# Where VectorE makes the split weights of the next chunk in a feed-forward network, and GpSimd's tall third parts in two operations

## The chip, the cores and the metric

The kernel runs on one core of one Trainium2 chip. The metric is the device time of one execution of the program in microseconds (us). The profile also gives the span (from the first to the last instruction in the trace), the busy time of each engine, and the clock that TensorE was granted, as a share of full speed.

The engines of the core work side by side, each in the order of its own instructions: TensorE (PE; its weight loads are shown apart as PEld), VectorE (DVE), ScalarE (ACT), GpSimd (POOL) and SyncE (SP), which issues most of the transfers. An instruction that needs another engine's result waits on a semaphore, and everything behind it in its own engine's order waits too.

## The reference, cut to what matters

A graph network on `x` of 1024 x 512 in fp32: a normalized and rectified `x` goes through a graph convolution (16384 edges), four layers of cross attention and a gated feed-forward network, and a second graph convolution, with residual sums. The change lies in the feed-forward network:

```python
N, D, BS, M, DC, H, DH, L, E = (1024, 512, 16, 256, 512, 8, 64, 4, 16384)
...
for i in range(L):
    a = _attn(_ln(h, ln2_w[i], ln2_b[i]), cond, Wq[i], Wk[i], Wv[i], Wo[i])
    h = h + a
    u = _ln(h, ln3_w[i], ln3_b[i]) @ geglu_w[i] + geglu_b[i]
    val, gate = jnp.split(u, 2, axis=-1)
    f = val * jax.nn.gelu(gate, approximate=False)
    h = h + f @ ffo_w[i] + ffo_b[i]
```

`geglu_w[i]` is 512 x 4096, so `val`, `gate` and `f` are 1024 x 2048; `ffo_w[i]` is 2048 x 512.

## The kernel before

**Tiling.** The large products are made by a scheme that needs seven block products where the plain one needs eight, at the price of sums and differences of blocks before and after. The products are numbered 0 to 6. The 2048 columns of `f` are worked off in four blocks r = 0 to 3 of 512 columns. Each block is made in four chunks c = 0 to 3 of 128 columns (the first product, with `geglu_w`), and later multiplied with its 512 rows of `ffo_w` in two output halves s = 0 and 1 (the second product).

**A chunk.** Block r = 0 is made in plain fp32 by another class. Blocks 1 to 3 use `Chunk` (from L1123), in which six of the seven products are made with split operands: each operand is written as a high part plus a low part in a narrower format (fp32r), and the product is the sum of three narrower ones. `split_left` (L1110) makes the three parts of a weight tile: the high part `gha` or `ghb` on ScalarE (L1112), the low part `gla` or `glb` on VectorE (L1113), and the third part, their difference, `gsa` or `gsb` on GpSimd (L1114). Each chunk has two such tiles: the tall one (names in a), 128 x 1024, holds the blocks of products 0, 5, 6 and 4; the low one (names in b), 128 x 512, those of products 1 and 3. `split(n, False)` splits the tall tile of the nth chunk ahead, `split(n, True)` its low tile. A chunk's weights arrive by transfers that SyncE issues when the chunk is made (L1137), and GpSimd builds the sums of its blocks (L1147, `sum_chunk`).

`Chunk.steps` is a generator that issues one chunk in stages. A product's first two parts are multiplied in `begin` (`gr` with `gha`, then `gl` with `gla`), the third part in `end` (`gr` with `gsa`), all by the matmuls at L1163. Between them ScalarE scales the bank in place (`scale`, L1177), or VectorE scales it and adds a term (`scale_onto`, L1181); VectorE adds (L1198), and ScalarE takes the GELU (L1190). The results go to `fT` (L1229, L1232). The fourth stage ends, in the kernel before, with a call of `split_low`, which the loop gives as `split(0, True)`.

**The right blocks.** The operand that all chunks share, the normalized `h`, is split as well. Its low parts `gl` are made by `finish_right` on VectorE (L1107), two operations for each product, during the last stage of r = 0.

**The output halves.** `Gated.sums` (L1302 to L1310) makes the sums and differences of the `fT` blocks for the second product (`fs`). `ffn_out` (L1320) then issues one half of the second product: seven products of eight matmuls each (L1333) into four banks of PSUM, `fa`, `fb`, `fc` and `fd`. VectorE adds them into the layer's sum `hall` (L1339) and into `kept`, a tile for each half that collects the terms common to several blocks (L1343 and L1351; for r = 0, ScalarE copies into it at L1345). The order is:

- TensorE: product 0 into `fa`, 6 into `fc`, 4 into `fd`, 5 into `fb`, 1 into `fa` again (onto what is there, in the same bank), 3 into `fc` and 2 into `fd`.
- VectorE: `kept` += `fa`, `hall` += `fc`, `hall` += `fd`, `kept` += `fb`, then `hall` += `fa`, += `fc`, += `fd`.

The second use of `fa` must wait until the first `kept` add has read it, that of `fc` until the first `hall` add has read that bank.

**The order of the work.** All of this is pinned: each engine works in the order in which the Python program issues its instructions. The loop over r = 1 to 3 and c = 0 to 3 interleaves the last stages of the chunk before with the first of this one. The two output halves of block r - 1 are issued behind the chunks c = 0 and c = 1 of the blocks r = 2 and 3, those of block 0 ahead of the loop, and those of block 3 in a last stage behind it, which the change doesn't touch. `out_weights` (L216 to L219) makes the sums of the `ffo_w` blocks on GpSimd once a block. SBUF slots and PSUM banks come from pools and are reused in order of allocation.

Of the kernel before, what the change touches and what calls it, by code (L numbers as in the profile page):

```python
# [11 lines left out]
F32R = mybir.dt.float32r  # L12
I32 = mybir.dt.int32
AF = mybir.ActivationFunctionType
OP = mybir.AluOpType
# [10 lines left out]
def gnn_kernel(  # L26
# [26 lines left out]
    nc = tc.nc  # L53
# [43 lines left out]
    def t512(name, dtype=F32):  # L97
        return work.tile([P, 512], dtype, tag="t512", name=name)

    def slot(name):  # L100
        return slots.tile([P, 2, 512], F32, tag="slot", name=name)
# [106 lines left out]
    h = [hall[:, nb, :] for nb in range(NB)]  # L208
# [76 lines left out]
    conds, left = {}, None  # L285
# [68 lines left out]
    at = 0  # L354
# [101 lines left out]
    def project_steps(nb, hT, w, name, emit):  # L456

        ph = bank(f"hw_{name}_{nb}")
        c0 = (nb % 4) * P
        for k in range(KC):  # L460
            nc.tensor.matmul(ph, hT[nb // 4][k // 2][:, k % 2, c0:c0 + P],
                             w[k // 2][:, k % 2, :], start=(k == 0), stop=(k == KC - 1),
                             skip_group_check=True)
            yield
        emit(nb, ph)
# [132 lines left out]
    def add_left(left, rows, to, root, name):  # L598

        for d in range(NB):  # L600
            nc.sync.dma_start(left.rearrange("p a b -> p (a b)"), left_dram[d])
            pl = bank(f"left_{name}_{d}")
            for s in range(NB):
# [7 lines left out]
    steps = (step for nb in range(NB)  # L611
             for step in project_steps(nb, h0T, w_in, "in",
                                       lambda nb, ph: nc.scalar.copy(hs_in[nb], ph)))
# [89 lines left out]
    def acc_tile(name):  # L703
        return accs.tile([P, 512], F32, tag="acc", name=name)
# [385 lines left out]
    pin = tc.keep_in_program_order  # L1090
# [19 lines left out]
    def split_left(x, h, l, s):  # L1110

        pin(nc.scalar.mul(h.bitcast(F32R), x, INWARD * TINY))  # L1112
        pin(nc.vector.scalar_tensor_tensor(l.bitcast(F32R), h, -1.0 / TINY, x, OP.mult, OP.add))  # L1113
        pin(nc.gpsimd.tensor_tensor(s.bitcast(F32R), h, l, OP.subtract))  # L1114

    def columns_of(t):
        return t.rearrange("p (b k c) -> p b k c", k=2, c=P)

    def flat(t):
        return t.rearrange("p a b -> p (a b)")  # L1120

    class Chunk:
# [26 lines left out]
        def split(self, low):  # L1149
            if low:  # L1150
                to = [t512(f"g{n}b_{self.n}") for n in "hls"]
            else:
                to = [flat(slot(f"g{n}a_{self.n}")) for n in "hls"]
            split_left(self.x[low], *to)
            self.parts[low] = [columns_of(t.bitcast(F32R)) for t in to]
# [33 lines left out]
            cg = self.cv + DFF // P  # L1189
            pin(nc.scalar.activation(to, of, AF.Gelu, bias=gcols[:, cg:cg + 1]))  # L1190

        def steps(self, sum_next, split_low):


            n, bias = self.n, gcols[:, self.cv:self.cv + 1]

            def add(to, x, y):
                pin(nc.vector.tensor_tensor(to, x, y, OP.add))  # L1198

            self.banks = {}  # L1200
            self.scale(0)
            self.scale(5)
            yield
            s1, u2, u3 = (acc_tile(f"g{x}_{n}") for x in ("s1", "u2", "u3"))
            pin(nc.scalar.copy(s1, self.end(0)))
            self.scale(6)
            yield
            add(u2, self.end(5), s1)
            yield
            sum_next()  # L1210
            self.scale(4)
            add(u3, self.end(6), u2)
            self.scale_onto(1, s1)
            g1 = acc_tile(f"g1_{n}")
            d = self.end(4)
            add(g1, d, u3)
            self.gate(g1, g1)
            self.scale_onto(3, u3)
            split_low()
            yield  # L1220
            a = self.end(1)
            yield
            g0 = acc_tile(f"g0_{n}")
            self.gate(g0, self.end(3))
            for k in range(2):
                pin(nc.tensor.matmul(d, self.last[:, k, :], self.rights[2][:, k, :], start=False,  # L1226
                                     stop=k == 1, skip_group_check=True))
            f0, f1 = self.f.of(self.c)
            pin(nc.vector.scalar_tensor_tensor(f0, a, bias, g0, OP.add, OP.mult))  # L1229
            add(d, d, u2)  # L1230
            yield
            pin(nc.vector.scalar_tensor_tensor(f1, d, bias, g1, OP.add, OP.mult))  # L1232

    class KeyPair(InStep):
# [3 lines left out]
        x = "k"  # L1238
# [78 lines left out]
        f = Gated(l, r)  # L1317
        return f, [Quad(l, r, c, left, right, f) for c in range(KC)]

    def ffn_out(l, r, s, left, right, kept, each=lambda ins: ins):  # L1320

        n = f"{l}_{r}_{s}"
        u = kept[s]
        a, b, c, d = (bank(f"{x}_{n}") for x in ("fa", "fb", "fc", "fd"))
        h11, h12, h21, h22 = (hall[:, 4 * i + 2 * s:4 * i + 2 * s + 2, j * M:(j + 1) * M]
                              for i in range(2) for j in range(2))

        def product(i, to, start):  # L1330
            for q in range(2):
                for k in range(2):
                    each(nc.tensor.matmul(to[:, q * M:(q + 1) * M],  # L1333
                                          left[i][k][:, (2 * s + q) * P:(2 * s + q + 1) * P],
                                          right[i][:, k, :], start=start and q == 0 and k == 0,
                                          stop=q == 1 and k == 1, skip_group_check=True))

        def add(to, of):
            each(nc.vector.tensor_tensor(to, halves_of(of), to, OP.add))  # L1339

        product(0, a, True)
        if r:
            each(nc.vector.tensor_tensor(u, a, u, OP.add))  # L1343
        else:
            nc.scalar.copy(u, a)  # L1345
        product(6, c, True)
        add(h22, c)
        product(4, d, True)
        add(h22, d)
        product(5, b, True)  # L1350
        each(nc.vector.tensor_tensor(u, b, u, OP.add))  # L1351
        if r == R - 1:
            for to in (h22, h21, h12):
                add(to, u)
        product(1, a, False)
        add(h11, a)
        product(3, c, False)
        add(h21, c)
        product(2, d, False)
        add(h12, d)  # L1360
# [43 lines left out]
    class QueryPair(InStep):  # L1404


        x = "q"
# [134 lines left out]
    for l in range(L):  # L1542

        wk, wv, wq, wo, ffb, spare = projections
        if l:
# [13 lines left out]
            kT_1, _ = keys(l, 1, wk)  # L1559
# [28 lines left out]
        ln3T, ln3S, right = [], [], []  # L1588
# [66 lines left out]
        for g in range(NG - 1):  # L1655
# [11 lines left out]
            if turn_two:  # L1667
                t = turn_next(g + 2)
# [19 lines left out]
            elif g:  # L1688
                turned = range(g) if g == NG - 2 else []
                if turned:  # L1690
                    with waiting_for(scores.last, mybir.EngineType.Pool):
                        left = geglu_weights(l, 0, *raw)
# [38 lines left out]
        f, quads = quads_of(l, 0, left, right)  # L1731
# [24 lines left out]
        kept = [t512(f"kept_{l}_{i}") for i in range(2)]  # L1756
# [7 lines left out]
        def finish_rights(*of):  # L1764
            for i in of:
                x, high, mid = begun[i]
                flow = finish_right(f"gl_{l}_{i}", x, high)
                Chunk.rights[i] = high, next(flow), mid
                yield
                for _ in flow:  # L1770
                    yield
# [13 lines left out]
        for c, q in enumerate(quads):  # L1785
            q.rest(fill)
            if c == 0:
                with waiting_for(q.last, mybir.EngineType.Pool):
                    wff = out_weights(nc.gpsimd, l, 0, raw_out)
# [10 lines left out]
        def sum_chunk(n):  # L1800
            if n < len(ready):
                ready[n].sums()
# [4 lines left out]

        load()
        sum_chunk(0)
        for _ in finish_rights(5, 6):  # L1810
            pass
        ffn_out(l, 0, 0, f.left(), wff, kept, pin)
        split(0, False)
        split(0, True)
        load()
        sum_chunk(1)
        for _ in finish_rights(4, 3):
            pass
        ffn_out(l, 0, 1, f.left(), wff, kept, pin)
        split(1, False)  # L1820
        load()
        raw_out = load_out(l, 1)

        def split_next(n):
            split(n, False)
            load()

        before = None
        for r in range(1, R):
            for c in range(KC):  # L1830
                chunk = ready.pop(0)
                flow = chunk.steps(lambda: sum_chunk(1), lambda: split(0, True))
                chunk.f = f if c else Gated(l, r)
                next(flow)
                if c > 2 or r == 1 and c or r > 1 and c == 0:
                    split_next(0)
                for step in range(3):
                    if before:
                        next(before, None)
                        if step == 2 and c == 0:  # L1840
                            f.sums(KC - 1, nc.vector, pin)
                    next(flow)
                if c:
                    f.sums(c - 1, nc.vector, pin)
                before = flow
                if c == 0:
                    kept_f, f = f, chunk.f
                if r > 1 and c < 2:
                    split_next(1)
                    ffn_out(l, r - 1, c, kept_f.left(), wff, kept, pin)  # L1850
                    if c == 1:
                        raw_out = load_out(l, r)
                if c == (KC - 1 if r + 1 < R else KC - 2):
                    wff = out_weights(nc.gpsimd, l, r, raw_out)
# [162 lines left out]
```

## Time and profile before

| | |
|---|---|
| median of three runs | 2477.06 us (2476.02 to 2477.70) |
| the profiled execution | 2477.45 us, its span 2475.6 us |
| mean granted TensorE clock over the span | 0.992 |
| ScalarE, high parts and scaling among it | 837.2 us busy, 34% |
| GpSimd | 1050.7 us busy, 1079 instructions |
| VectorE's `gla` (L1113), 48 in all | 85.6 us busy, 1784 ns each |
| memory traffic | 138.12 MB read, 23.07 MB written, 65 GB/s over the span |

The page of the profile begins with the busy time of each engine and its share of the span; behind the x is the number of instructions. In a view of waits, a row such as `PE fa L1333 <- DVE kept L1343: 37.8, 8, 4.7` says that TensorE's instructions that write `fa` at line 1333 waited for VectorE's `kept` of line 1343, 37.8 us in total, in 8 waits, the longest of them 4.7. In a timeline, a row gives the start, the duration, the engine, the line, the operation, output and inputs, the shape, how many instructions stand in the row (x8), and in brackets how long its engine idled before it and what ended this. Where a row stands for several matmuls its duration runs from the first's start to the last's end. In a view of windows, a row gives for each stretch its length, the busy time of each engine with the number of instructions, the granted clock (PEclk), and the share and rate of the transfers.

### The profile page before, as it was taken

Reading aid. Unit: us, or ns where it says so; the run is one execution under the profiler, and the core shown is the slowest. Engines: PE = TensorE matmul, PEld = TensorE weight load, DVE = VectorE, ACT = ScalarE, POOL = GpSimd, SP = SyncE. Lnnn points to the kernel's source line nnn. Section 1 sums busy time; section 2 is a strip of 40 time slices with the busy share of each in tenths; the row PEclk is TensorE's granted clock in tenths of the full one; section 3 lists DMA queues with packets and bytes.
Section 4 is the critical chain, followed back from the end, with each engine's and each line's share of the span. In section 5 each row is a group of like instructions: output and inputs, shape, how many; then the busy total and the mean of one; then the engine's idle time right before and its main releaser. Section 6 shows DMA issues by size and latency. Waiting matters only on the chain. (4 is left out here: it accounts for less than half of the span.)

```text
span 2475.6 us, 35108 instructions
## 1 busy us (share of the span) xinstructions
PE 2401.2 (97%) x13032; PEld 1883.8 (76%) x13032; DVE 1701.2 (69%) x3252; ACT 837.2 (34%) x1784; POOL 1050.7 (42%) x1079
## 2 busy tenths in 40 slices
PE   8999999999999999999999999999999999999999
PEld 5778886677787887577787888477787888667787
DVE  9665666877676557886686556776785556777764
ACT  7323344333213334343213334432323333433220
POOL 0433444564453222574453224554544322555531
PEclk9999999999999999999999999999999999999999
DMA  5323220111302220021221221011131031011140
GB/s 178 122 68 116 90 95 18 43 43 52 119 31 77 87 74 20 22 64 43 62 96 69 77 72 41 9 60 43 43 132 69 14 124 48 5 52 39 47 145 35
DMA packets 118065, 163.55 MB, mean 66 GB/s; under 512 B 9256, under 2 KB 66928, under 8 KB 117888
## 3 DMA queue, kind: packets, MB, share of 16 engines
q1 hardware_dynamic: 115792, 155.81, 19.1%
q0 software_dynamic: 1376, 4.30, 0.5%
q8 instruction: 107, 1.75, 0.3%
q10 hardware_dynamic: 720, 1.11, 0.1%
q14 instruction: 70, 0.57, 0.1%
HBM read 138.12 MB, written 23.07 MB: 65 GB/s over the span
## 5 line engine op out<-in xcount | busy, mean ns | idle before, releaser
L1177 ACT ACTIVATE g<-g 128x512 f32<-128x512 f32 x192 | 112.1, 584 | 312.6 <-PE g L1163 308.8
L1114 POOL TENSOR_TENSOR gsb<-ghb,glb 128x512 fp32r<-128x512 f32 x48 | 74.2, 1545 | 240.6 <-DVE glb L1113 240.6
L1333 PE MATMUL fa<-wff,fT 128*128 128x256 f32 x512 | 135.2, 410 | 37.8 <-DVE kept L1343 37.8
L1114 POOL TENSOR_TENSOR gsa<-gha,gla 128x1024 fp32r<-128x1024 f32 x48 | 115.0, 2396 | 111.9 <-DVE gla L1113 111.9
L1333 PEld LDWEIGHTS fa<-wff,fT 128*128 128x128 f32 x512 | 105.1, 207 | 61.1 <-DVE kept L1343 41.0
L799 ACT ACTIVATE pr<-sc,nmax 128x256 f32<-128x256 f32 x256 | 118.2, 471 | 83.1 <-DVE nmax L794 82.6
L1163 PE MATMUL g<-gr,gsa 128*128 128x512 f32 x384 | 136.6, 437 | 0.0
L1003 POOL TENSOR_TENSOR kr<-ct,ct 128x256 f32<-128x256 f32 x48 | 36.8, 766 | 211.8 <-DVE pr L804 207.2
L1190 ACT ACTIVATE g<-g,gcols 128x512 f32<-128x512 f32 x96 | 67.4, 703 | 168.8 <-DVE g L1198 165.6
L300 PE MATMUL pa_v<-wv,ct 128*128 128x256 f32 x512 | 124.0, 385 | 0.0
L1163 PE MATMUL g<-gr,gha 128*128 128x512 f32 x384 | 122.7, 401 | 0.0
L300 PE MATMUL pc_v<-wv,ct 128*128 128x256 f32 x512 | 121.0, 379 | 0.0
L300 PE MATMUL pd_v<-wvs,ct 128*128 128x256 f32 x512 | 121.0, 379 | 0.0
L1163 PE MATMUL g<-gl,gla 128*128 128x512 f32 x384 | 118.6, 390 | 0.0
L794 DVE TENSOR_REDUCE nmax<-sc 128x2 f32<-128x512 f32 x128 | 83.7, 679 | 41.2 <-PE sc L787 41.2
L300 PEld LDWEIGHTS pa_v<-wv,ct 128*128 128x128 f32 x512 | 94.9, 190 | 22.5 <-issue 9.2
L300 PEld LDWEIGHTS pd_v<-wvs,ct 128*128 128x128 f32 x512 | 97.3, 190 | 13.2
L300 PEld LDWEIGHTS pc_v<-wv,ct 128*128 128x128 f32 x512 | 97.0, 190 | 13.0
L1113 DVE SCALAR_TENSOR_TENSOR gla<-gha,gxa 128x1024 fp32r<-128x1024 f32 x48 | 85.6, 1784 | 18.0 <-ACT gha L1112 18.0
L1163 PEld LDWEIGHTS g<-gr,gsa 128*128 128x128 f32 x384 | 71.9, 188 | 33.5 <-issue 16.3
L1229 DVE SCALAR_TENSOR_TENSOR fT<-g,gcols,g 128x512 f32<-128x512 f32 x48 | 35.9, 749 | 80.1 <-ACT g L1190 79.8
L1226 PE MATMUL g<-ln3T,gy 128*128 128x512 f32 x192 | 90.4, 592 | 0.0
(520 smaller groups left out, 6357.5 us busy)
## 6 DMA issues: line engine op xcount, KB each, us to landing
ct<-cond_dram SPq DMA_DIRECT2D x72, 512.0 KB, 5.6
wff<-in_L_gnn_ffo_w_dram SPq DMA_DIRECT2D x32, 512.0 KB, 3.9
cond_dram<-ct SPq DMA_DIRECT2D x24, 512.0 KB, 3.0
gxb<-in_L_gnn_geglu_w_dram SPq DMA_DIRECT2D x96, 128.0 KB, 2.2
gxa<-in_L_gnn_geglu_w_dram SPq DMA_DIRECT2D x96, 128.0 KB, 2.3
cond<-in_L_gnn_cond_dram SPq DMA_DIRECT2D x32, 256.0 KB, 4.7
ct<-cond_dram SPq DMA_DIRECT2D x24, 256.0 KB, 5.6
wk<-in_L_gnn_Wk_dram SPq DMA_DIRECT2D x8, 512.0 KB, 6.3
```

What stands on the lines that cost most here:

```text
L300: each(nc.tensor.matmul(at, left[:, k, l0:l1], right[:, k, r0:r1], start=start and n == 0 and k == 0, stop=n == len(cols_of) - 1 and k == ...
L794: nc.vector.tensor_reduce(nmax, ps3, AX.X, OP.max, negate=True)
L799: nc.scalar.activation(pr3[:, a, :], ps3[:, a, :], AF.Exp, bias=nmax[:, a:a + 1], accum_out=tot[:, a:a + 1])
L1003: t.tensor_tensor(to, of, less, OP.subtract)
L1113: pin(nc.vector.scalar_tensor_tensor(l.bitcast(F32R), h, -1.0 / TINY, x, OP.mult, OP.add))
L1114: pin(nc.gpsimd.tensor_tensor(s.bitcast(F32R), h, l, OP.subtract))
L1163: pin(nc.tensor.matmul(to, self.part(i, which)[:, k, :], self.rights[i][which].bitcast(F32R)[:, k, :], start=start and k == 0, stop=stop a ...
L1177: pin(nc.scalar.mul(to, to, 1.0 + TINY))
L1190: pin(nc.scalar.activation(to, of, AF.Gelu, bias=gcols[:, cg:cg + 1]))
L1226: pin(nc.tensor.matmul(d, self.last[:, k, :], self.rights[2][:, k, :], start=False, stop=k == 1, skip_group_check=True))
L1229: pin(nc.vector.scalar_tensor_tensor(f0, a, bias, g0, OP.add, OP.mult))
L1333: each(nc.tensor.matmul(to[:, q * M:(q + 1) * M], left[i][k][:, (2 * s + q) * P:(2 * s + q + 1) * P], right[i][:, k, :], start=start and q ...
```

## The change

It has four parts.

1. `split_left`: GpSimd makes the third part in column blocks of 512. For the low tile that is one operation as before; for the tall tile, two of 128 x 512 in place of one of 128 x 1024. That adds 48 instructions on GpSimd. ScalarE's and VectorE's operations on the tall tile stay whole.
2. `ffn_out` takes a sequence `beside` of functions. The first is called after VectorE's second `kept` add (for r = 3 after the adds of `u`, too), ahead of product 1; the others after `hall` += `fa`, ahead of product 3.
3. Block r = 0: the right blocks of product 6 are finished inside the first half instead of ahead of it, those of 3 inside the second half, both with the splits that stood behind these halves; those of product 4 are finished inside the second half instead of ahead of it, and only those of product 5 still come ahead of the first.
4. Blocks r = 2 and 3, chunks c = 0 and 1: `split(0, True)` is no longer called in the fourth stage of the chunk, and `split_next(1)` no longer ahead of `ffn_out`; both go into `ffn_out` as `beside`. In all other chunks `split(0, True)` is called at the same place as before.

The instructions of TensorE, ScalarE and SyncE stand in the same order before and after. On VectorE 17 operations a layer stand elsewhere (11 of L1113 and 6 of L1107); on GpSimd, `gsa` and `gsb` follow them, in two pieces where tall.

```diff
@@ split_left
-        pin(nc.gpsimd.tensor_tensor(s.bitcast(F32R), h, l, OP.subtract))
+        for at in range(0, x.shape[-1], 512):
+            h_at, l_at, s_at = (t[:, at:at + 512] for t in (h, l, s.bitcast(F32R)))
+            pin(nc.gpsimd.tensor_tensor(s_at, h_at, l_at, OP.subtract))
@@ Chunk.steps
-        def steps(self, sum_next, split_low):
+        def steps(self, sum_next):
...
             self.scale_onto(3, u3)
-            split_low()
             yield
@@ ffn_out
-    def ffn_out(l, r, s, left, right, kept, each=lambda ins: ins):
+    def ffn_out(l, r, s, left, right, kept, each=lambda ins: ins, beside=()):
...
         if r == R - 1:
             for to in (h22, h21, h12):
                 add(to, u)
+        for do in beside[:1]:
+            do()
         product(1, a, False)
         add(h11, a)
+        for do in beside[1:]:
+            do()
         product(3, c, False)
@@ ahead of the loop (r = 0)
-        for _ in finish_rights(5, 6):
-            pass
-        ffn_out(l, 0, 0, f.left(), wff, kept, pin)
-        split(0, False)
-        split(0, True)
+        def finish(*of):
+            for _ in finish_rights(*of):
+                pass
+
+        def split_both():
+            split(0, False)
+            split(0, True)
+
+        finish(5)
+        ffn_out(l, 0, 0, f.left(), wff, kept, pin, (lambda: finish(6), split_both))
         load()
         sum_chunk(1)
-        for _ in finish_rights(4, 3):
-            pass
-        ffn_out(l, 0, 1, f.left(), wff, kept, pin)
-        split(1, False)
+        ffn_out(l, 0, 1, f.left(), wff, kept, pin,
+                (lambda: finish(4), lambda: (finish(3), split(1, False))))
@@ the loop over r and c
-                flow = chunk.steps(lambda: sum_chunk(1), lambda: split(0, True))
+                flow = chunk.steps(lambda: sum_chunk(1))
...
+                output = r > 1 and c < 2
+                if not output:
+                    split(0, True)
                 if c:
                     f.sums(c - 1, nc.vector, pin)
...
-                if r > 1 and c < 2:
-                    split_next(1)
-                    ffn_out(l, r - 1, c, kept_f.left(), wff, kept, pin)
+                if output:
+                    ffn_out(l, r - 1, c, kept_f.left(), wff, kept, pin,
+                            (lambda: split(0, True), lambda: split_next(1)))
```

## The prediction

> **What bounds the kernel now.** I read the page's first two parts, then the list of TensorE's own waits, then the timelines around the longest of them. All times are from the one profiled execution, which took 2477.45 us (its span 2475.6, 1.85 around it); the median of the runs is 2477.06, 0.39 less.
>
> ```profile
> span 2475.6 us, 35108 instructions
> PE 2401.2 (97%) x13032; PEld 1883.8 (76%) x13032; DVE 1701.2 (69%) x3252; ACT 837.2 (34%) x1784; POOL 1050.7 (42%) x1079
> ...
> PE fa L1333 <- DVE kept L1343: 37.8, 8, 4.7
> PE fd L1333 <- DVE fs L1309: 8.7, 11, 0.9
> PE fc L1333 <- DVE hall L1339: 4.7, 4, 1.2
> ```
>
> TensorE is busy 97% of the span: only what shortens its idle time, or the stretches in which it runs slowly, can count. Its longest wait by far (total, times, longest) is in the output halves: 37.8 us in 8 waits, before the second product into `fa`, on VectorE's `kept` add. Eight is one in each of r = 2 and 3 in four layers: the half that follows chunk c = 0. The next view is the timeline of TensorE there (start, duration), with the half after c = 1 below it:
>
> ```profile
> 539.32 1.56 PE L1333 MATMUL fd<-wffs,fs 128*128 128x256 f32 x6 [0.94 <-DVE fs L1309]
> 540.72 1.89 PE L1333 MATMUL fb<-wffs,fs 128*128 128x256 f32 x8
> 547.34 3.78 PE L1333 MATMUL fa<-wff,fT 128*128 128x256 f32 x8 [4.72 <-DVE kept L1343]
> 555.10 0.81 PE L1163 MATMUL g<-gr,gha 128*128 128x512 f32 x2
> ...
> 572.17 1.89 PE L1333 MATMUL fa<-wff,fT 128*128 128x256 f32 x8
> 573.90 1.89 PE L1333 MATMUL fc<-wffs,fT 128*128 128x256 f32 x8
> 577.17 0.81 PE L1163 MATMUL g<-gr,gha 128*128 128x512 f32 x2
> ```
>
> The wait costs more than its 4.72 us: the eight matmuls into `fa` behind it take 3.78 instead of 1.89. From `fa` to the next chunk's first matmul it is 7.76 us here and 5.00 after c = 1, where nothing waits. The granted clock (PEclk) tells why:
>
> ```profile
> core 0: us, PE busy (x) PEld busy (x) DVE busy (x) ACT busy (x) POOL busy (x), PEclk, DMA share, GB/s
> 544.60:545.60 1.00, 0.00 (x0) 0.00 (x0) 1.00 (x1) 0.00 (x0) 1.00 (x1) 1.00 0.00 0
> 545.60:546.60 1.00, 0.00 (x0) 0.00 (x0) 1.00 (x1) 0.00 (x0) 0.00 (x0) 0.67 0.00 0
> 546.00:547.34 1.34, 0.00 (x1) 0.01 (x1) 1.34 (x3) 0.00 (x0) 0.52 (x1) 0.50 0.00 0
> ...
> 572.17:577.17 5.00, 5.00 (x26) 4.40 (x24) 2.14 (x4) 0.00 (x0) 2.67 (x4) 1.00 0.38 148
> ```
>
> A mean of 0.67 over 545.60 to 546.60 means half speed from about 545.9 on, some 3.3 us after TensorE ran dry at 542.6. The same stretch, `fa` to next chunk, over all eight halves (first, last, sum; the columns are its ends, its length, TensorE's busy time, PEclk and DMA):
>
> ```profile
> 547.34:555.10 7.76, 7.76 (x25) 0.65 0.00 0
> ...
> 2341.77:2348.32 6.55, 6.55 (x24) 0.77 0.00 0
> sum 54.78, PE 54.78; mean PE 6.85
> ```
>
> **The change, part by part.** It adds no work but 48 instructions on GpSimd (each tall third part becomes two); TensorE, ScalarE and SyncE keep their order, VectorE has 17 operations a layer in other places.
>
> *1. `kept` first, in r = 2 and 3.* What VectorE (and GpSimd) did before the late add:
>
> ```profile
> 541.52 0.68 DVE L1198 TENSOR_TENSOR g<-g,gu 128x512 f32<-128x512 f32 x1
> 542.12 0.68 DVE L1181 SCALAR_TENSOR_TENSOR g<-g,gu 128x512 f32<-128x512 f32 x1
> 543.57 0.69 DVE L1113 SCALAR_TENSOR_TENSOR glb<-ghb,gxb 128x512 fp32r<-128x512 f32 x1 [0.76 <-ACT ghb L1112]
> 544.51 2.17 DVE L1113 SCALAR_TENSOR_TENSOR gla<-gha,gxa 128x1024 fp32r<-128x1024 f32 x1 [0.25 <-ACT gha L1112]
> 546.60 0.68 DVE L1343 TENSOR_TENSOR kept<-fa,kept 128x512 f32<-128x512 f32 x1
> ...
> 544.34 1.26 POOL L1114 TENSOR_TENSOR gsb<-ghb,glb 128x512 fp32r<-128x512 f32 x1 [2.55 <-DVE glb L1113]
> ```
>
> The two splits (`glb`, `gla`) and their waits for ScalarE stand between L1181 and `kept`. Both now come later. Operations of this size follow at 0.60 us (541.52, 542.12), so `kept` starts at 542.12 + 0.60 = 542.72 instead of 546.60: 3.88 us earlier, 8 times, **31.0 us**. What is late next: `kept` ends 0.68 later, TensorE could have started at 542.45 (`fb` begins at 540.72, and groups of eight follow at 1.73: 572.17, 573.90), so about 0.84 of the 4.72 stays.
>
> *2. The slow clock.* A wait of 0.84 us ends 2.4 us before the 3.3 at which the clock fell. The waits of 0.94 (`fd` above) and 1.18 (below) were followed by groups of eight at 1.89 and 1.99 us. I take the slow stretch as gone: 54.78 - 8 x 5.00 = **14.8 us**; the other bound is 0.
>
> *3. r = 0.* In the second half of r = 0 VectorE made `gl` for products 4 and 3 ahead of the half's adds:
>
> ```profile
> 475.30 1.89 PE L1333 MATMUL fc<-wff,fT 128*128 128x256 f32 x8
> 483.55 1.99 PE L1333 MATMUL fc<-wffs,fT 128*128 128x256 f32 x8 [1.18 <-DVE hall L1339]
> ...
> 476.12 6.77 DVE L1107 SCALAR_TENSOR_TENSOR gl<-ln3S,gr 128x512 fp32r<-128x512 f32 x4
> 482.82 0.68 DVE L1339 TENSOR_TENSOR hall<-fc,hall 128x512 f32<-128x512 f32 x1
> ```
>
> With them behind the adds, the add of `fc` can run at 475.30 + 1.89 = 477.2, five us before TensorE wants `fc` back (483.55 - 1.18 = 482.37). The wait goes, in four layers: **4.7 us**. `gl` for product 4 now follows `fb`, which is done at 475.30 + 2 x 1.73 + 1.89 = 480.7; two operations of 0.60, or of 1.7 if hindered as in the row (6.77 / 4), end by 484.1, and the next chunk starts only at 482.37 + 2 x 1.73 = 485.8. The splits of r = 0's first half move ahead of its last two adds; nothing on TensorE waits for these.
>
> *4. Tall third parts in two.* [...]
>
> ```profile
> 535.24 2.35 POOL L1114 TENSOR_TENSOR gsa<-gha,gla 128x1024 fp32r<-128x1024 f32 x1
> 535.32 2.82 DVE L1308 TENSOR_TENSOR fs<-fT,fT 128x512 f32<-128x512 f32 x1
> 538.17 1.10 DVE L1309 TENSOR_TENSOR fs<-fs,fT 128x512 f32<-128x512 f32 x1
> ...
> L1114 POOL TENSOR_TENSOR gsa<-gha,gla x48: 2348/2374/2667, 475.7 to 2363.6; 128x1024 fp32r<-128x1024 f32 x48
> L1114 POOL TENSOR_TENSOR gsb<-ghb,glb x48: 1260/1607/1715, 478.4 to 2382.8; 128x512 fp32r<-128x512 f32 x48
> ```
>
> `gsb` is the nearest row to a half of `gsa`: 1.26 to 1.71 us, so a pair is 2.52 to 3.43 against 2.37 (0.15 to 1.06 more, 48 times, on an engine 42% busy). The first `fs` then waits for the first half only: it ends at 535.24 + 1.26 + 0.60 = 537.1 instead of 538.1; the second `fs` meets the second half (to 537.1 + 1.26 = 538.4) and ends near 539.0 instead of 539.27. I take 0.2 us of this as reaching `kept`, 8 times, **1.6 us**. Bounds: 1.09 each, the full difference of 2.35 and 1.26 (8.7 us), and, if both halves go first, a loss of 2.52 - 2.35 = 0.17 each (1.4 us).
>
> [...]
>
> *What hides the moved work.* The tall part is due late, and the banks as well:
>
> ```profile
> 519.53 2.38 POOL L1114 TENSOR_TENSOR gsa<-gha,gla 128x1024 fp32r<-128x1024 f32 x1 [1.16 <-DVE gla L1113]
> 526.66 0.62 PE L1163 MATMUL g<-gr,gsa 128*128 128x512 f32 x2
> ...
> 560.44 0.75 DVE L1229 SCALAR_TENSOR_TENSOR fT<-g,gcols,g 128x512 f32<-128x512 f32 x1 [4.26 <-ACT g L1190]
> 561.60 0.63 PE L1163 MATMUL g<-gr,gha 128*128 128x512 f32 x2
> 570.16 0.68 DVE L1343 TENSOR_TENSOR kept<-fa,kept 128x512 f32<-128x512 f32 x1
> ```
>
> In an ordinary chunk `gsa` is done 4.75 us before its matmul: a pair costs at most 1.06 of it. In a half after c = 0, VectorE's new order is `kept` (542.72), two adds, the second `kept`, `glb`, an add (five steps of 0.60 to 0.70 from 543.3, so to 546.7), `gla`, two adds. `gla` waits for `gsb`, which can start at 546.0 and takes up to 1.71, and itself takes 1.1 (2.17 less the 1.09 that `gsb` held it above): to 548.8, and the adds to about 550.1. The next chunk starts at 543.46 + 5.00 = 548.46, 1.6 us earlier. VectorE is idle for 4.26 there, and the fourth bank of that chunk (product 4, 561.60 - 555.10 = 6.5 us in) is the first that needs one of them. After c = 1, `kept` ends at 570.84 and TensorE comes for it at 572.17: no wait to gain. SyncE's loads in the moved step keep their place in its queue, and what they fill is first used a chunk later. All this I cost at nothing.
>
> Sum: 31.0 + 14.8 + 4.7 + 1.6 = 52.1; 2477.45 - 52.1 = 2425.35, and 0.39 less for the median: **2425 us**.
>
> **The rivals.** *The clock stays slow.* The halves still hold two short waits (0.94 and 0.84) within four us. If these keep the clock down, part 2 is lost: 2425 + 14.8 = 2440. For it: they come closer together than any waits in the rows above. Against it: each alone left the pace unchanged. [...]
>
> *`kept` doesn't come earlier*, because something else on VectorE holds it (its input `fa` is complete before `fd` resumes at 539.32, so I see nothing). Only part 3 is left: 2477.06 - 4.7 = 2472, which is at the edge of what a measurement tells from no change (0.2%, 5 us).
>
> *Slower: the adds behind `gla` come too late.* The place is the first matmul of product 4 after each of the 16 changed halves of r = 2 and 3. If a backlog keeps the last adds from ending within 6.5 us of the chunk's start, TensorE waits there; a wait like today's costs 4.72 + 14.8 / 8 = 6.6 us with its slow clock. 16 x 6.6 = 105 us: 2425 + 105 = 2530. From 3.3 us a half on it eats the gain. Against it: the backlog I find is 1.6 us.
>
> **How the numbers follow.** Forecast 0.78; clock stays slow 0.11; nothing but part 3, 0.04; slower 0.07. Faster is the first two, 0.89; the same 0.04. The forecast's own range is 2425 - (8.7 - 1.6) = 2418 to 2425 + 1.6 + 1.4 = 2428. For eight in ten the first rival is taken in: 2417 to 2441.
>
> **What would show it.** Right: the wait of `fa` on `kept` falls from 4.7 to about 0.8 each; the stretch `fa` to next chunk is 5.0 in all eight halves, with PEclk 1.00; the wait of `fc` on `hall` is gone; `gsa` x96 at 1.26 to 1.71; the first `fs` ends after some 1.8 instead of 2.82. Wrong: PEclk below 1 in these halves (first rival), a new wait of a `g` product on `hall` or on `gsa` (third), or `kept` still starting 4 us after the last L1181.

## The result, and the profile after

The changed kernel takes 2421.68 us (median; 2421.45 to 2422.37) against 2476.70 us for the kernel before: a ratio of 0.9778, with a 95% interval of 0.9761 to 0.9795. The forecast was 2425, with a range of 2417 to 2441.

The page of the profile after, its first lines:

```profile
span 2419.5 us, 35192 instructions
PE 2385.1 (99%) x13032; PEld 1874.2 (77%) x13032; DVE 1665.3 (69%) x3252; ACT 838.0 (35%) x1784; POOL 1050.1 (43%) x1127
```

The span is 56.1 us shorter. TensorE's idle time went from 74.4 us (2475.6 - 2401.2) to 34.4, its busy time from 2401.2 to 2385.1: 40.0 us of waits and 16.1 us of slow work. The list of TensorE's waits of the kernel after begins with:

```profile
PE fa L1334 <- DVE kept L1344: 6.7, 8, 0.8
PE fd L1334 <- DVE fs L1310: 4.4, 11, 0.4
```

`fa` on `kept` fell from 37.8 to 6.7, `fd` on `fs` from 8.7 to 4.4, and `fc` on `hall` (4.7) is not in the list any more: 40.1 us together, all of the idle time that went. The timeline of TensorE in the second half of r = 0, where nothing waits any more, and in the first changed half of r = 2:

```profile
479.75 1.89 PE L1334 MATMUL fa<-wff,fT 128*128 128x256 f32 x8
481.47 1.89 PE L1334 MATMUL fc<-wffs,fT 128*128 128x256 f32 x8
...
536.59 1.56 PE L1334 MATMUL fd<-wffs,fs 128*128 128x256 f32 x6 [0.40 <-DVE fs L1310]
537.99 1.89 PE L1334 MATMUL fb<-wffs,fs 128*128 128x256 f32 x8
540.71 1.99 PE L1334 MATMUL fa<-wff,fT 128*128 128x256 f32 x8 [0.83 <-DVE kept L1344]
545.81 0.81 PE L1165 MATMUL g<-gr,gha 128*128 128x512 f32 x2
```

The wait in the changed half is 0.83 where it was 4.72, and the eight matmuls into `fa` take 1.99 where they took 3.78. The windows from `fa` to the next chunk, in the same eight halves as before (first and last: ends, length, TensorE's busy time, granted clock, transfers):

```profile
540.71:545.81 5.10, 5.10 (x24) 1.00 0.00 0
...
2287.17:2292.27 5.10, 5.10 (x24) 1.00 0.00 0
sum 40.79, PE 40.77; mean PE 5.10
```

The clock is 1.00 in all eight, and the sum went from 54.78 to 40.79: 14.0 of the 16.1 us. Most of the rest lies at the start of the program, ahead of all that was changed: from 27.0 to 30.5 us the clock was 0.52 in the profiled execution before and 1.00 in this one. VectorE's timeline shows where the rest of its work went:

```profile
533.12 1.74 DVE L1309 TENSOR_TENSOR fs<-fT,fT 128x512 f32<-128x512 f32 x1
534.90 1.64 DVE L1310 TENSOR_TENSOR fs<-fs,fT 128x512 f32<-128x512 f32 x1
...
539.39 0.68 DVE L1183 SCALAR_TENSOR_TENSOR g<-g,gu 128x512 f32<-128x512 f32 x1
539.99 0.67 DVE L1344 TENSOR_TENSOR kept<-fa,kept 128x512 f32<-128x512 f32 x1
...
542.57 0.68 DVE L1113 SCALAR_TENSOR_TENSOR glb<-ghb,gxb 128x512 fp32r<-128x512 f32 x1
543.17 0.68 DVE L1340 TENSOR_TENSOR hall<-fa,hall 128x512 f32<-128x512 f32 x1
543.77 1.90 DVE L1113 SCALAR_TENSOR_TENSOR gla<-gha,gxa 128x1024 fp32r<-128x1024 f32 x1
545.60 0.68 DVE L1340 TENSOR_TENSOR hall<-fc,hall 128x512 f32<-128x512 f32 x1
546.20 0.69 DVE L1340 TENSOR_TENSOR hall<-fd,hall 128x512 f32<-128x512 f32 x1
551.11 0.75 DVE L1230 SCALAR_TENSOR_TENSOR fT<-g,gcols,g 128x512 f32<-128x512 f32 x1 [4.22 <-ACT g L1192]
```

`kept` follows the last scaling at 0.60 us. The splits come behind it, and VectorE is through at 546.89, with 4.22 us idle ahead of its next work.

### The profile page after: what moved, and what is told of

Its sections match the earlier page's. It is cut to its first block, busy times and chain, and to the rows that moved or that the text cites. A ratio compares the mean times of both kernels' runs of the same rounds, so it can differ in the third digit from the quotient of the medians.

```text
span 2419.5 us, 35192 instructions
## 1 busy us (share of the span) xinstructions
PE 2385.1 (99%) x13032; PEld 1874.2 (77%) x13032; DVE 1665.3 (69%) x3252; ACT 838.0 (35%) x1784; POOL 1050.1 (43%) x1127
## 5 line engine op out<-in xcount | busy, mean ns | idle before, releaser
L1116 POOL TENSOR_TENSOR gsa<-gha,gla 128x512 fp32r<-128x512 f32 x96 | 126.1, 1336 | 103.5 <-DVE gla L1113 103.5
L1334 PE MATMUL fa<-wff,fT 128*128 128x256 f32 x512 | 122.4, 381 | 6.7 <-DVE kept L1344 6.7
L1334 PEld LDWEIGHTS fa<-wff,fT 128*128 128x128 f32 x512 | 96.5, 190 | 26.9 <-DVE kept L1344 9.9
L897 POOL TENSOR_TENSOR ou<-ou 128x256 f32<-128x256 f32 x12 | 8.7, 727 | 190.4 <-DVE ou L896 127.4
```

The source lines that it names most:

```text
L1116: pin(nc.gpsimd.tensor_tensor(s_at, h_at, l_at, OP.subtract))
L1334: each(nc.tensor.matmul(to[:, q * M:(q + 1) * M], left[i][k][:, (2 * s + q) * P:(2 * s + q + 1) * P], right[i][:, k, :], start=start and q ...
```

## The experiments

The kernel before, timed beside the experiments, took 2476.84 us beside the four kernels with parts alone, 2476.69 beside those with one and two extra operations, and 2476.96 beside all others.

### The parts alone

**Third parts whole again** (all other parts of the change kept):

```diff
-        for at in range(0, x.shape[-1], 512):
-            h_at, l_at, s_at = (t[:, at:at + 512] for t in (h, l, s.bitcast(F32R)))
-            pin(nc.gpsimd.tensor_tensor(s_at, h_at, l_at, OP.subtract))
+        pin(nc.gpsimd.tensor_tensor(s.bitcast(F32R), h, l, OP.subtract))
```

> The changed kernel with GpSimd's tall third part whole again (one operation of 128x1024). If halving it is what shortened the wait of fd on fs (from 0.94 to 0.40 us in eight halves, 4.3 us in the list of waits), the wait is 0.94 again and the time 2421.7 + 4.3 = 2426.0 us. Rival: the halving did nothing and the sums come earlier because the splits in front of them moved; then the wait stays near 0.4 and the time at 2421.7 us. In the forecast this part was worth 1.6: 2423.3 us.

Measured: 2426.57 us (2425.51 to 2427.40), 4.9 more than the changed kernel. Its list of TensorE's waits:

```profile
PE fd L1332 <- DVE fs L1308: 8.8, 11, 0.9
PE fa L1332 <- DVE kept L1342: 6.7, 8, 0.8
```

The wait of `fd` on `fs` is back at its old size, and that of `fa` stayed: the halving is worth 4 to 5 us here, by way of `fs`, as expected; the rival falls.

**Only the moves in r = 2 and 3**: third parts whole, and block r = 0 as in the kernel before.

```diff
-        finish(5)
-        ffn_out(l, 0, 0, f.left(), wff, kept, pin, (lambda: finish(6), split_both))
+        for _ in finish_rights(5, 6):
+            pass
+        ffn_out(l, 0, 0, f.left(), wff, kept, pin)
+        split(0, False)
+        split(0, True)
...
```

> The changed kernel with only the moves in r = 2 and 3 (third parts whole, block r = 0 as before). If the terms add: 2476.7 - 31.1 (idle time of fa) - 14.0 (slow stretch) = 2431.6 us, PEclk 1.00 in the eight stretches. Rival, that the moves in r = 0 or the halving are needed for the clock to stay up: PEclk below 1 in some of them, and up to 2445.6 us.

Measured: 2432.69 us (2431.62 to 2433.20), 44.2 less than before, with the clock at 1.00 in the eight stretches (sum 40.78). These moves alone stop the slow stretches. And the step from this kernel to the one with r = 0 moved as well is 2432.69 - 2426.57 = 6.1 us: that is what r = 0 is worth.

**Only r = 0**, and **only the halving**, each put into the kernel before (the hunks are those of the change):

> The kernel before with only the moves in block r = 0. By the comparison of the two traces these halves are 1.46 us shorter in each layer (1.18 of it the wait of fc on hall): 2476.7 - 5.8 = 2470.9 us, with no wait of fc on hall. Rival: the wait goes, but the gl operations of the products 3 and 4, which now come behind the adds, hold up the first chunk of r = 1; then a new wait of a g product on gl stands there and the time stays within 1 us of 2476.7.

> The kernel before with only the halving of GpSimd's tall third part. If the terms add, the time is 2476.7 - 4.3 = 2472.4 us: fd waits 0.4 us for fs in the halves after c = 0, and fa still 4.7 us for kept. Rival: VectorE, half a microsecond earlier there, waits that much longer for ScalarE's ghb (0.76 us before), so that kept starts at its old time: fd's wait falls, fa's grows by the same, and the time stays at 2476.7 us.

Measured: 2473.62 us (2472.06 to 2475.11) and 2474.60 us (2472.10 to 2476.83): gains of 3.2 and 2.2 us, where 5.8 and 4.3 were expected; the ratio of the halving alone, 0.9991, has an interval of 0.9981 to 1.0001, so that its own gain isn't settled by the times. The rivals are not the reason. With only r = 0 moved, the wait of `fc` is gone and none on `gl` stands in the list. With only the halving, VectorE's timeline ahead of `kept` has:

```profile
542.85 0.69 DVE L1113 SCALAR_TENSOR_TENSOR glb<-ghb,gxb 128x512 fp32r<-128x512 f32 x1 [0.76 <-ACT ghb L1112]
```

The wait for `ghb` is 0.76 as before: ScalarE moved along. And the halving does more than was expected, as it also shortens the wait in r = 0:

```profile
PE fc L1335 <- DVE hall L1341: 2.5, 4, 0.6
```

That is 2.2 us less for `fc` (4.7 before), beside 4.3 less for `fd`. What ate the gain is in the windows from `fa` to the next chunk:

```profile
546.62:553.95 7.33, 7.33 (x25) 0.69 0.00 0
...
sum 58.64, PE 58.63; mean PE 7.33
```

The same waits of 4.72 us as before are followed by slow stretches of 58.64 us in sum where the kernel before had 54.78; with only r = 0 moved they are 56.21. For the halving that makes 4.3 + 2.2 - 3.9 = 2.6 us, and the two spans differ by 2.4. For r = 0 it makes 5.8 - 1.4 = 4.4; the spans differ by 3.9 and the times by 3.2, which is within the spread of the runs. TensorE's work in these stretches and the wait ahead of them are the same in the three kernels; what differs is when they come. The next experiments tell why that can matter.

### How long a wait the clock bears

The changed kernel with n extra operations on VectorE ahead of the first `kept` add in the eight halves, n = 1, 2, 3 and 6 (the maximum of `kept` with itself, which leaves it as it is):

```diff
         if r:
+            for _ in range(n if len(beside) and s == 0 else 0):
+                each(nc.vector.tensor_tensor(u, u, u, OP.max))
             each(nc.vector.tensor_tensor(u, a, u, OP.add))
```

Three and six ran first:

> The changed kernel with three extra operations on VectorE (the maximum of kept with itself, 128x512, which leaves it as it is) ahead of the first kept add in the eight halves after c = 0. They follow at 0.60 us, so fa waits 0.83 + 1.80 = 2.63 us there. Theory: the clock falls only about 3.3 us after TensorE ran dry, so the pace behind the wait stays (PEclk 1.00, some 5.1 us from fa to the next chunk) and the time is 2421.7 + 8 x 1.80 = 2436.1 us. Rival: each idle time slows the stretch behind it in proportion (14.0 us for eight waits of 4.72 us): 8 x 1.75 x 1.80 / 3.89 = 6.5 us more, 2442.6 us.

> The same with six extra operations: fa waits 0.83 + 3.60 = 4.43 us. Theory: beyond 3.3 us the clock falls, and the stretch from fa to the next chunk is long again (6.2 to 6.9 us, PEclk 0.65 to 0.80): 2421.7 + 28.8 + 11 to 14 = 2461 to 2465 us. Rival: the slow stretch of the kernel before came from its two splits and from GpSimd beside them, not from the idle time; then the stretch stays at 5.1 us and the time is 2421.7 + 28.8 = 2450.5 us.

Then, with a new theory, one and two:

> The changed kernel with one extra operation ahead of the first kept add in the eight halves after c = 0; three took 0.75 us each, so fa waits 0.83 + 0.75 = 1.58 us. New theory, from the runs with waits of 3.08, 4.72 and 5.26 us: the clock is decided at the ends of fixed stretches of 3.41 us, and falls for the next one if TensorE was idle for more than about 1.9 us of such a stretch. A wait of 1.58 us can't fill it: PEclk 1.00 in all eight, and the time is 2421.7 + 8 x 0.75 = 2427.7 us, the same in every execution within 1 us. The prediction's theory (the clock falls 3.3 us after TensorE ran dry) says the same.

> The same with two extra operations: fa waits 0.83 + 1.50 = 2.33 us. New theory: the wait slows what follows where at least 1.9 us of it fall into one fixed stretch of 3.41 us, which a wait of 2.33 does in some (2.33 + 3.41 - 2 x 1.9) / 3.41 = 0.57 of its positions: four or five of eight halves slow, 1.5 to 1.8 us each, and different ones in each execution: 2433.7 to 2448 us, most near 2441, with a spread of several us between executions. The prediction's theory (3.3 us after TensorE ran dry): none slow, 2421.7 + 8 x 1.50 = 2433.7 us in all executions.

| n | wait of `fa`, us | slow stretches of eight | their sum, us | time, us |
|---|---|---|---|---|
| 0 (the changed kernel) | 0.83 | 0 | 40.79 | 2421.68 |
| 1 | 1.63 | 0 | 40.78 | 2428.55 (2427.28 to 2429.63) |
| 2 | 2.35 | 8 | 54.28 | 2445.55 (2444.64 to 2447.91) |
| 3 | 3.08 | 5 | 50.22 | 2449.39 (2448.63 to 2451.11) |
| 6 | 5.26 | 8 | 56.30 | 2472.43 (2471.77 to 2475.39) |

The extra operations cost about 0.75 us each and not 0.60, so the waits are longer than planned for three and six. In each kernel the added waits and the longer stretches make up the added time to within 2 us (n = 6: 8 x 4.43 + 15.5 = 50.9, measured 50.8).

With six, the splits stand behind `kept`, GpSimd is idle during the wait (8.01 us ahead of `gsb`), and all eight stretches are slow: the rival that the splits caused the slow clock falls. The time of 2461 to 2465 us was missed since each wait is 5.26 us long and not 4.43. With three, both theories are wrong. With waits of 3.08 us, below the 3.3 of the prediction, five stretches are slow; and they are not slower in proportion, but either 5.1 us long or 6.6 to 7.9. The windows of the kernel with three operations, cut at the places where its clock changes and at whole multiples of 3.413 us from there (PEclk, the granted clock, is the third column from the right):

```profile
core 0: us, PE busy (x) PEld busy (x) DVE busy (x) ACT busy (x) POOL busy (x), PEclk, DMA share, GB/s
538.25:541.67 3.42, 1.98 (x10) 1.40 (x8) 3.38 (x6) 1.76 (x3) 1.77 (x3) 1.00 0.00 0
541.67:545.08 3.41, 1.77 (x8) 1.59 (x9) 3.17 (x6) 0.43 (x1) 0.00 (x0) 1.00 0.00 0
545.08:548.49 3.41, 3.41 (x19) 3.00 (x17) 3.41 (x5) 0.00 (x0) 1.34 (x2) 1.00 0.00 0
1104.87:1108.28 3.41, 0.33 (x2) 0.24 (x2) 3.24 (x6) 1.96 (x3) 0.00 (x0) 1.00 0.00 0
1108.28:1111.69 3.41, 3.41 (x9) 2.70 (x9) 2.23 (x5) 0.00 (x0) 1.03 (x1) 0.50 0.02 5
...
1173.13:1176.55 3.42, 1.56 (x8) 1.03 (x6) 3.35 (x6) 2.18 (x3) 1.35 (x2) 1.00 0.00 0
1176.55:1179.96 3.41, 2.19 (x10) 1.96 (x11) 3.20 (x6) 0.01 (x1) 0.00 (x0) 1.00 0.00 0
...
1739.75:1743.16 3.41, 1.36 (x7) 0.85 (x5) 3.34 (x6) 2.19 (x3) 1.15 (x2) 1.00 0.00 0
1743.16:1746.57 3.41, 2.38 (x6) 1.93 (x7) 3.20 (x6) 0.00 (x0) 0.00 (x0) 0.50 0.00 0
1746.57:1749.99 3.42, 3.42 (x10) 2.70 (x9) 1.98 (x3) 0.00 (x0) 1.27 (x2) 0.50 0.00 0
```

The changes of the clock lie on one grid of 3.413 us: 1743.16 - 1108.28 = 634.88 = 186 times it. In the trace of the kernel before, the clock is 0.50 from 27.11 to 30.52 us, one such stretch, and falls for the last time at 2474.46, 717 times 3.413 behind the first. Where the wait is split by a line of the grid (541.67, 1176.55), neither stretch is idle enough, and the clock stays: idle 1.44 and 1.64, then 1.86 and 1.22 (3.41 or 3.42 less the busy time). Where most of it falls into one stretch (1104.87: idle 3.08; 1739.75: idle 2.05), the whole next stretch runs at 0.50. A slow stretch with 1.03 us idle is followed by another slow one. The same cut in the kernel with two operations, where 2.36 us of one stretch were idle:

```profile
540.67:544.09 3.42, 1.06 (x5) 0.83 (x5) 3.18 (x6) 2.03 (x3) 0.02 (x1) 1.00 0.00 0
544.09:547.50 3.41, 3.41 (x10) 2.71 (x9) 2.98 (x5) 0.00 (x0) 1.27 (x1) 0.50 0.00 0
```

So the second theory, idle time within a fixed stretch, holds in these kernels with a bound between 1.86 and 2.05 us. Two other kernels narrow it: with only r = 0 moved, 3.41 - 1.52 = 1.89 us idle kept the clock once (from 1757.75), and in the kernel with twelve operations, below, 3.42 - 1.46 = 1.96 dropped it (from 1807.35). One stretch of the last doesn't fit: 3.41 - 1.70 = 1.71 us idle was enough there (from 1172.47), where 3.42 - 1.67 = 1.75 elsewhere in the same kernel was not (from 2312.52). Why is open.

The second theory forecast the kernel with one operation (2427.7) to within 0.9 us, with no slow stretch. With two it gave the time's range (2433.7 to 2448) and the old theory's 2433.7 fell; but all eight halves were slow and not four or five. The chance of 0.57 for each took the positions as independent, and they aren't: from the first `fa` (543.18) to the second (612.17) it is 68.99 us, 20.21 stretches, and from there to the third (1109.81) 497.64, 145.79 stretches, so a half that was slow brings the one after next into the same position. That this is why all eight fell is worked out and wasn't tried.

### How much VectorE can be late behind the splits

Twelve extra operations of the same kind behind the moved splits, in the 16 halves of r = 2 and 3:

```diff
         for do in beside[1:]:
             do()
+        for _ in range(12 if r and len(beside) else 0):
+            each(nc.vector.tensor_tensor(u, u, u, OP.max))
         product(3, c, False)
```

> The changed kernel with twelve extra operations on VectorE (the maximum of kept with itself) behind the moved splits in the 16 halves of r = 2 and 3, ahead of the last two hall adds: 7.2 us at 0.60, up to some 10 where GpSimd's third parts hold them up. The last add after c = 0, which ends at 546.89 us in the changed kernel, then ends at 554.1 to 556.6, and the next chunk's fourth bank is due 6.5 us after its start at 545.81, at 552.3. Theory of the third rival's place: TensorE waits there, 1.8 to 4.3 us in the eight halves after c = 0 and less after c = 1, where VectorE is idle: 2436 to 2470 us. Rival theory: what the adds hold up is due earlier (a bank of the chunk's first three products), and the wait is longer and stands at its start: above 2480 us.

Measured: 2523.32 us (2523.04 to 2524.75), 101.6 more than the changed kernel. Its list of waits:

```profile
PE g L1165 <- DVE hall L1340: 55.3, 16, 4.7
PE g L1165 <- ACT g L1179: 12.6, 8, 1.7
```

VectorE's timeline in the first of these halves:

```profile
545.71 12.29 DVE L1363 TENSOR_TENSOR kept<-kept 128x512 f32<-128x512 f32 x12
557.92 0.68 DVE L1340 TENSOR_TENSOR hall<-fc,hall 128x512 f32<-128x512 f32 x1
```

And TensorE's:

```profile
545.91 0.82 PE L1165 MATMUL g<-gr,gha 128*128 128x512 f32 x2
...
558.65 1.22 PE L1165 MATMUL g<-gr,ghb 128*128 128x512 f32 x2 [3.34 <-DVE hall L1340]
```

The mechanism of the third rival is real, and the sixteen halves cost about what it put on them (105 us), though by other terms: 55.3 us of waits for `hall`, 12.6 of new waits for ScalarE's `g`, and 32.9 of slow work. Its place was wrong: the matmul that waits is the first with the low tile (`ghb`, product 1), which TensorE reaches at 558.65 - 3.34 = 555.31, 9.4 us into the chunk and not 6.5, and what it waits for is the add of `fc`. In the changed kernel that add ends at 545.60 + 0.68 = 546.28, and 9.4 us into the chunk is 545.81 + 9.4 = 555.2: 8.9 us to spare. The twelve took 12.29 us, 1.02 each and not 0.60. That is 3.4 more than the 8.9 to spare, as the row's 3.34 shows. The time lies in the range of the rival theory (a bank that is due earlier), but the place speaks against it: the bank is due later than was thought. The time is that long since the waits came in all 16 halves, and TensorE's busy time grew from 2385.1 to 2418.0 (96% of its span), 32.9 us; its mean clock was 0.988 where the changed kernel had 1.00.

### A version that beats both

In the chunks c = 0 of r = 2 and 3, two of VectorE's operations of the chunk's tail, and ScalarE's GELU between them, come behind the first adds of the half:

```diff
-            add(g1, d, u3)
-            self.gate(g1, g1)
-            self.scale_onto(3, u3)
+            to = self.begin(3)
+
+            def late():
+                add(g1, d, u3)
+                self.gate(g1, g1)
+                pin(nc.vector.scalar_tensor_tensor(to, to, 1.0 + TINY, u3, OP.mult, OP.add))
...
         add(h22, d)
+        late()
         product(5, b, True)
```

All other chunks call `late` at the old place.

> The changed kernel, and in the chunks c = 0 of r = 2 and 3 two of VectorE's operations of the chunk's tail (the add that makes the gate's input, and the scaling of product 3 with its term) come after the kept and hall adds of fa, fc and fd instead of ahead of them. Then the first kept add starts 1.20 us earlier, and fa's wait of 0.83 us in eight halves goes: 2421.7 - 6.7 = 2415.0 us. Rival: the two operations, now 1.8 us later, delay ScalarE's gate and high parts and with them the moved splits; then a wait of the next chunk's product 3 or 4 takes the place, and the time is 2421.7 us or more.

Measured: 2412.70 us (2412.32 to 2413.65), a ratio of 0.9739 to the kernel before (0.9722 to 0.9756), and 9.0 less than the changed kernel, where 6.7 were expected. The rival's wait of a `g` product isn't in its list of waits. VectorE's timeline:

```profile
540.01 0.67 DVE L1349 TENSOR_TENSOR kept<-fa,kept 128x512 f32<-128x512 f32 x1
...
541.99 0.68 DVE L1200 TENSOR_TENSOR g<-g,gu 128x512 f32<-128x512 f32 x1
542.59 0.69 DVE L1223 SCALAR_TENSOR_TENSOR g<-g,gu 128x512 f32<-128x512 f32 x1
```

TensorE's:

```profile
539.21 1.89 PE L1339 MATMUL fb<-wffs,fs 128*128 128x256 f32 x8
540.93 1.89 PE L1339 MATMUL fa<-wff,fT 128*128 128x256 f32 x8
```

`fa` follows `fb` by 540.93 - 539.21 = 1.72 us, where it came 540.71 - 537.99 = 2.72 behind it in the changed kernel. So the wait of 0.83 cost more than its row says: groups of eight overlap by 0.16 where nothing waits (1.89 long, 1.73 apart), and that was lost too. With the group itself back at 1.89 from 1.99, a half gains 0.99 + 0.10 = 1.09 us, and eight 8.7, about the 9.0 between the times. The two spans differ by 7.6 only, since this profiled execution is behind before anything differs: its first changed `fb` starts 1.22 us later than the changed kernel's (539.21 against 537.99), with a clock of 0.53 from 27.0 to 30.5 us where the other had 1.00.

## Why the prediction was right, point by point

- **`kept` first: 31.0 us forecast, 31.1 measured** (37.8 to 6.7). The start after the last scaling at 0.60 and the remaining 0.84 came out as worked out.
- **The slow clock: 14.8 forecast, 14.0 measured.** The stretches are gone, at 5.10 us each and not 5.00: the group behind a short wait takes 1.99, which the prediction's own row of `fc` showed and its sum left out. The reason given was wrong in its bound. In these kernels the clock does not fall 3.3 us after TensorE ran dry. It falls at the end of a fixed stretch of 3.413 us in which TensorE was idle for at least some 1.9 us (once 1.7). The 3.3 came from the first of the eight waits, and windows of the same trace, the one before the change, speak against it:

```profile
542.52:545.93 3.41, 0.09 (x1) 0.00 (x0) 2.39 (x3) 1.96 (x3) 1.26 (x1) 1.00 0.00 0
614.20:617.61 3.41, 1.31 (x7) 0.81 (x5) 2.39 (x5) 2.19 (x3) 0.86 (x2) 1.00 0.00 0
617.61:621.02 3.41, 0.78 (x2) 0.69 (x3) 3.31 (x4) 0.00 (x0) 2.19 (x2) 0.50 0.00 0
```

  The first wait happened to begin 0.09 us into a stretch, so that 3.3 us of it were left. In the second half TensorE ran dry at 614.20 + 1.31 = 615.51, and the clock fell at 617.61, 2.1 us later. The remaining 0.83 us is below either bound, and the other ground given, that waits of 0.94 and 1.18 had left the pace alone, was sound, so the result held; had 2.35 remained, the step would have said "no loss", and the runs show eight slow stretches.
- **r = 0: 4.7 forecast, 6.1 measured** by two kernels that differ in it alone. The wait of `fc` (4.7) is gone, its four groups take 1.89 where they took 1.99 (0.4), and the overlap of 0.16 with the group ahead, which a wait ends, is back (4 x 0.16 = 0.6). The prediction counted the wait alone; from `fa` to `fd` it is 1.35 + 0.10 = 1.45 us less in each layer (480.48 to 485.38 before, 479.75 to 483.20 after), 5.8 in four.
- **Tall third parts in two: 1.6 forecast, 4.3 measured** in the list of waits, 4.9 in the times. This is the term that was mis-sized most; it is small, and lay within its bounds. The first `fs` fell from 2.82 to 1.74 as said. That it would end soon behind GpSimd's operation was the prediction's estimate from one pair of rows, and the two traces bear it out: the median of that line's 28 is 0.69 us in both, and this one took 2.82 beside the whole `gsa` (2.35) and 1.74 beside the first half (1.27). The second was thought to lose most of that again, with GpSimd's second half taking a whole 1.26 us from the end of the first `fs`. GpSimd's timeline after shows:

```profile
533.04 1.27 POOL L1116 TENSOR_TENSOR gsa<-gha,gla 128x512 fp32r<-128x512 f32 x1
534.26 1.72 POOL L1116 TENSOR_TENSOR gsa<-gha,gla 128x512 fp32r<-128x512 f32 x1
```

  The row of the second half begins before the first `fs` ends (534.86) and ends at 535.98, 1.12 us behind it. The second `fs` ended at 536.54, 3.42 us after the first `fs` began, against 538.17 + 1.10 - 535.32 = 3.95 in the kernel before: 0.53 us in each of eight halves reach TensorE, and not 0.2.
- **What hides the moved work: right, with more room than said.** The moved `gla` took 1.90 us, the adds ended 1.1 us into the next chunk (546.89 - 545.81) and not 1.6, and the time to spare was 8.9 us. SyncE's and GpSimd's orders brought no new wait.
- **The rivals.** The clock didn't stay slow (1.00 in all eight). `kept` did come earlier. The late adds need a backlog of 8.9 us, where the prediction had the point product 4, 6.5 us into the chunk; at 12.29 us they cost 101.6 us.

The terms as measured, 31.1 + 14.0 + 5.8 + 4.3, make 55.2; the medians differ by 55.0. The forecast of 52.1 put the two small terms 1.1 and 2.7 too low and the slow clock 0.8 too high, so that a part of the errors cancelled.

## What to carry to other kernels

An operation on the path between two engines should come ahead of work that is only due later, and how much later is read from the first instruction that waits for it, not from the first that could. A wait of a few microseconds on TensorE costs its length, here some 0.3 us more in lost overlap (0.16) and a slower first group (0.10), and in some places (all eight waits of 2.35 us, five of eight of 3.08) a slow stretch behind it; so a saving is worked out for all of these, and a wait that is cut to half its length (4.72 to 2.35 us here) may still cost the clock. Small gains measured alone, with such waits still standing, can vanish in part in where the slow stretches fall: the same two parts gave 3.2 and 2.2 us before the waits were cut, and 6.1 and 4.9 after.

## What the runs showed of the hardware that was not expected

- TensorE's granted clock was 1.00 or 0.50 in every stretch of 3.413 us read here, and it changed at the ends of these, by what was idle in the stretch before: idle 1.89 us kept it once (only r = 0 moved), 1.71 dropped it once (twelve operations), and 1.96 us or more always did in the rows read here, and a slow stretch with 1.03 us idle (three operations) was followed by another. A wait of 3.08 us was free of it in three halves of eight, one of 2.35 us in none.
- Operations of 128x512 on VectorE that read and write the same tile one after the other cost 0.75 us each (waits of `fa` of 0.83, 1.63, 2.35 and 3.08 for 0 to 3 of them), where the others follow at 0.60; beside GpSimd's third parts and sums, 1.02 on average (12.29 for twelve). Whether the shared tile is the reason was not tried.
- A wait costs TensorE more than its row: groups of eight matmuls that follow at 1.73 us lose 0.16 of overlap, and the group behind the wait takes 1.99 where it takes 1.89 otherwise.
